# A graph-attention kernel: the values' stride in the second layer, the accumulator's second half in the third

## The chip, the core and the metric

The program runs on one NeuronCore of a Trainium2 chip. The metric is the device time of one execution in microseconds; the median of three runs is compared. A profiled execution of the same program supplies the trace. Its engines are named PE (TensorE, matmuls) with PEld (its weight loads), DVE (VectorE), ACT (ScalarE), POOL (GpSimd) and SP (SyncE, which here only issues transfers).

## What is computed

4096 nodes with 256 features each and a 0/1 adjacency matrix of 4096 x 4096 go through three graph-attention layers, a dense block of 30 steps after the first of them, and a mixture of experts at the end:

```python
x = x + _L0_gnn_ref(_layernorm(x), adj, W, a1, a2)          # attention, layer 1
x = x + _L0_ffn_ref(_layernorm(x), ...)                     # 30 dense steps
x = x + _L1_gnn_ref(t, _layernorm(x), adj, W1, a1, W2, a2)  # attention, layers 2 and 3
x = x + _L1_ffn_ref(_layernorm(x), ...)                     # experts, top 2 of 6
```

One attention layer, for each of four heads of 64 columns:

```python
h = jnp.einsum('nf,hfd->hnd', x, W)
f1 = jnp.einsum('hnd,hd->hn', h, a[:, :D])
f2 = jnp.einsum('hnd,hd->hn', h, a[:, D:])
e = jax.nn.leaky_relu(f1[:, :, None] + f2[:, None, :], ALPHA)
e = jnp.where(adj[None, :, :] > 0, e, NEG)
att = jax.nn.softmax(e, axis=-1)
out = jax.nn.elu(jnp.einsum('hnm,hmd->hnd', att, h))
```

## The kernel before

The leaky relu has two branches, and the exponential of a sum is a product. So the softmax-weighted sum over the neighbours m of a node n splits into two sums: one over the neighbours with f1 + f2 above zero, one over those below it. Each neighbour contributes a factor that depends on m alone, which is multiplied into its values beforehand, and a factor of n alone, which is applied at the end. What is left for the matmuls is to add up rows of values under two 0/1 masks, "above" and "below".

**Values.** The tile `vals` holds, for each block j of 128 neighbours and each head h, two parts (above and below). A part is 130 numbers of 16 bits: 65 high halves (64 columns and the denominator) and 65 low halves, which together carry more precision than one 16-bit number. Its shape before is [128, 32, 4, 2, 2, 65] (DV = 65). A part is therefore 260 bytes long, the parts lie end to end, and the second begins 260 bytes after the first. `upper` writes the high halves (ACT, L378), `lower` the low halves (DVE, L383).

**Masks.** For each block of neighbours ACT or DVE compares f1 with f2 (L462, L460) into the tile `st`. DVE then ANDs `st` with the adjacency mask (L568), which makes the mask "above", and XORs the result with the adjacency mask (L574), which makes `below`. All of these are 8-bit.

**Products (L520).** The nodes of a layer are worked in four chunks of 1024, which is 8 tiles of 128 nodes, each with its own PSUM bank of 512 numbers. A unit is one chunk, one head and four neighbour blocks. In a unit, and for each of two groups of four banks, the loop runs over the four blocks s, the four tiles i, and the two parts. Each pass loads a mask of 128 x 128 as weights and streams one part's 130 columns of values:

```python
for i in range(n):
    ...
    for part in range(2):
        cols = slice(2 * part * DV, 2 * (part + 1) * DV)
        nc.tensor.matmul(
            acc[:, i, cols], masked[part][:, at_i // TR, s, rows], v[:, cols], ...
```

So part 0 (weights `st`) goes to columns 0 to 129 of bank i, part 1 (weights `below`) to columns 130 to 259, and then the next bank follows. Each layer has 128 units of 64 matmuls: 8192 matmuls, half of them of each part. After eight units a head of a chunk is finished; `lower_sums` (ACT, L469) and `whole_sums` (DVE, L473) read the banks through the view `split`, and `close` (DVE mostly, L483 to L498) finishes the output.

**Order.** In the stage with the products, the instructions of DVE and ACT stand in the order of the program's text (`manual_schedule`). The preparation before it (the layer's projections, its scores, the values) is ordered by the scheduler, from its own estimates and from which memory is free. SP issues the loads in one queue: 1 MB adjacency masks (L193), rows of the layer's input into the tile `ring` (L93), scores (L188, L348), and stores of outputs (L628).

**Memory.** `vals` comes from a pool that is opened after a few small ones, and the pools for masks, f1, steps, work and outputs lie above it. Layers 2 and 3 open the same pools in the same order at the same addresses, so that in the kernel before a tile of layer 3 lies where the same tile of layer 2 was. The dense block, which stands between layers 1 and 2, has its own pools in the same memory.

Of the kernel before, what the change touches and what calls it, by code (L numbers as in the profile page):

```python
# [13 lines left out]
F16 = mybir.dt.float16  # L14
# [9 lines left out]
P = 128  # L24
C = 256
KC = C // P
H = 4
# [7 lines left out]
DV = D + 1  # L35
# [11 lines left out]
def gnn_ffn_kernel(ctx: ExitStack, tc: tile.TileContext, a: dict, out: bass.AP):  # L47
# [3 lines left out]
    NT = N // P  # L51
# [106 lines left out]

        return w, (load, make, centre)

    def attention(tag, src, norm, w, front, chunks, first, ends, following, side={}):

# [4 lines left out]
        with ExitStack() as scope:  # L169
# [2 lines left out]
            nf2 = lay.tile([P, NT, H], F32, name="nf2")  # L172
            hs = lay.tile([P, 1, H, DV], F32, name="hs")
            end = None if first else scope.enter_context(tc.tile_pool(name=f"{tag}_end", bufs=1))
            vals = scope.enter_context(tc.tile_pool(name=f"{tag}_vals", bufs=1)).tile(
                [P, NT, H, 2, 2, DV], F16, name="vals"
            )
            mask = [scope.enter_context(tc.tile_pool(name=f"{tag}_mask", bufs=4))]
            fpool = scope.enter_context(tc.tile_pool(name=f"{tag}_f", bufs=2))

# [55 lines left out]
            with ExitStack() as ps:  # L236
# [164 lines left out]
                for g in range(NG + 2):  # L401
                    if g + 2 < NG:
                        load(g + 2)
                    if 2 <= g < NG:
                        columns(g)
                    if 1 <= g <= NG:
                        now = products(g - 1)
                    if 2 <= g:
                        lower(g - 2)
                    if g < 2:  # L410
                        columns(g)
                    if g in (0, 2) and late:
                        late.pop(0)()
                    if 1 <= g <= NG:
                        upper(g - 1, *now)
                    if first:
                        for n in range(PREP * g // 8, min(PREP * (g + 1) // 8, PREP)):
                            make_piece(n)
                    elif g in (2, 4, 6):
                        load_mask(0, g // 2)  # L420
# [41 lines left out]
                    nc.scalar.activation(out, f1, AF.Sign, bias=f2, scale=-1.0)  # L462

            def split(acc, n):
                return acc[:, :n, : 4 * DV].rearrange("p i (b s c) -> p i b s c", b=2, s=2)

            def lower_sums(i0, n, acc):
                lo = end.tile([P, 4, 2, DV], F32, name="lo", bufs=2)
                nc.scalar.activation(lo[:, :n], split(acc, n)[:, :, :, 1, :], AF.Copy, scale=1.0 / LOW)  # L469
                return lo  # L470

            def whole_sums(u, lo, i0, n, acc):
                nc.vector.tensor_tensor(  # L473
                    u[:, i0 : i0 + n], split(acc, n)[:, :, :, 0, :], lo[:, :n], OP.add
                )
# [28 lines left out]
            pairs = {}  # L504

            def products(at, k):


                c, h, q = units[at]
                masked = pairs[at]  # L510
                for s in range(JU):
                    j = JU * q + s
                    v = vals[:, j, h].rearrange("p b s c -> p (b s c)")
                    i0, n, acc = accs[c, h][k]
                    for i in range(n):
                        at_i = (i0 + i) * P
                        rows = slice(at_i % TR, at_i % TR + P)
                        for part in range(2):
                            cols = slice(2 * part * DV, 2 * (part + 1) * DV)
                            nc.tensor.matmul(  # L520
                                acc[:, i, cols],
                                masked[part][:, at_i // TR, s, rows],
                                v[:, cols],
                                start=(j == 0 and part == 0),
                                stop=(j == NT - 1 and part == 1),
                                skip_group_check=True,
                            )
# [10 lines left out]
            with tc.manual_schedule(engines={mybir.EngineType.DVE, mybir.EngineType.Activation}):  # L538
# [3 lines left out]
                for at in range(len(units) + LAG):  # L542
                    b = at - LAG
# [4 lines left out]
                    if at < len(units):  # L548
                        c, h, q = units[at]
# [26 lines left out]
                    if b >= 0:  # L576
                        for k in range(2):
                            if bq == 0:
                                space(bc, bh, k)
                            products(b, k)  # L580
                        pairs.pop(b)
                        if not first and bh == H - 1 and bq % 2 == 1 and bc + 1 < len(chunks):
                            load_mask(bc + 1, bq // 2)
                        if 0 < bq < 7 and closing is not None:
                            next(closing)
# [16 lines left out]
            c, h, q = units[-1]  # L602
# [6 lines left out]
    def to_rows(dst, src=None):  # L609


        def block(x, t, n, h):
            return x[t * P : (t + n) * P, h * D : (h + 1) * D].rearrange("(r p) d -> p r d", p=P)

        def begin(t, n, h, work):
            if src is not None:
                old = work.tile([P, 4, 2, DV], F32, name="old", tag="lo", bufs=2)
                old = old.rearrange("p i b c -> p (i b c)")[:, : 8 * D].rearrange("p (i d) -> p i d", d=D)
                nc.sync.dma_start(old[:, :n], block(src, t, n, h))
                return old[:, :n]  # L620

        def finish(t, n, h, u, e, old):
            if src is None:
                nc.vector.tensor_scalar(u, u, 0.0, -1.0, op0=OP.max, op1=OP.add)
            else:
                nc.vector.scalar_tensor_tensor(u, u, 0.0, old, op0=OP.max, op1=OP.add)
            made = nc.vector.scalar_tensor_tensor(e, e, 1.0, u, op0=OP.min, op1=OP.add)
            nc.sync.dma_start(block(dst, t, n, h), e)  # L628
            return made

        return begin, finish
# [106 lines left out]
    first = ctx.enter_context(tc.tile_pool(name="f_first", bufs=4))  # L738
# [49 lines left out]
    def front(prep, small_ps):  # L788
# [12 lines left out]
    side = {  # L801
        31: [(begin_weights, 1)],
        28: [(load, g) for g in range(3)],
        26: [(make_weights, 1, 0)],
        22: [(make_weights, 1, 1)],
        20: [(load, 3)],
        18: [(measure, 0)],
        14: [(measure, 1)],
        10: [(rate, 0), (rate, 1)],
        4: [(measure, 2)],  # L810
        1: [(measure, 3), (init, 0), (init, 1), (rate, 2), (rate, 3)],
    }
    attention(
        "g0",
        x,
# [176 lines left out]
    def centre_weights(prep, small_ps):  # L992
        layers[1][1][2](small_ps)

    side = {
        k: functools.partial(many, v)
        for k, v in {24: (begin_weights, 2), 14: (make_weights, 2, 0), 10: (make_weights, 2, 1)}.items()
    }
    for n in range(2):
        attention(  # L1000
            f"g{n + 1}",
            h1d if n else x2d,
            not n,
            layers[n + 1][0],
            None if n else centre_weights,
            [8, 8, 8, 8],
            False,
            to_rows(x3d, x2d) if n else to_rows(h1d),
            [NG // 2, x3d, runs_of] if n else [2, h1d],
            {} if n else side,  # L1010
        )


# [5 lines left out]
    with ExitStack() as scope:  # L1019
# [4 lines left out]
        acc = one.tile([P, NT, C], F32, name="acc")  # L1024
# [256 lines left out]
        with tc.tile_pool(name="r_ps", bufs=1, space=PSUM) as psum, tc.tile_pool(  # L1281
            name="r_pst", bufs=4, space=PSUM
# [11 lines left out]
            for i in range(3):  # L1294
                src = a[f"L1_ffn_expert_w{i + 1}"]
# [173 lines left out]
```

## Time and profile before

| | us |
|---|---|
| median of 3 runs (2987.83 to 2989.67) | 2988.52 |
| profiled execution: its own time | 2978.01 |
| profiled execution: span of the trace | 2976.1 |
| products of layer 1, first to last start (L520) | 93.2 to 599.4 |
| products of layer 2 | 1624.2 to 2112.0 |
| products of layer 3 | 2166.4 to 2652.4 |
| experts, after layer 3 | 2652 to 2976 |

The span is the distance from the first to the last instruction of the trace. The dense block and the preparation of layer 2 fill the time from 600 to 1624 us, and the preparation of layer 3 the 54 us between the products of layers 2 and 3. Over the whole span PE is busy for 94%, DVE for 92% and ACT for 83%, but these are averages over stages with different limits, so each stage has to be read by itself. The mean granted TensorE clock is 0.979 of full speed; it is 1.00 in the middle of each attention layer.

### The profile page before, as it was taken

How to read it: one execution, taken by the hardware profiler on the slowest of the kernel's cores; microseconds unless marked ns; L12 is line 12 of the kernel's file. 1: busy time of each engine (PE TensorE's matmuls, PEld its weight loads, DVE VectorE, ACT ScalarE, POOL GpSimd, SP SyncE). 2: the span in 40 equal slices, each digit the busy share in tenths (PEclk: the TensorE clock that was granted, in tenths of full speed). 3: DMA queues.
4: the chain of work that ended last, by engine and by line, in shares of the span. 5: the costliest groups of instructions: out<-in, count | busy, mean ns of one | idle time of the engine just before them, and what ended most of it. 6: DMA issues, size and time to landing. Idle time of an engine off the chain costs nothing. (4 is left out here: it accounts for less than half of the span.)

```text
span 2976.1 us, 82659 instructions
## 1 busy us (share of the span) xinstructions
PE 2800.0 (94%) x33923; PEld 2562.3 (86%) x33923; DVE 2740.5 (92%) x5769; ACT 2465.1 (83%) x3125; POOL 1157.6 (39%) x1084
## 2 busy tenths in 40 slices
PE   7899999979999999999998999999889999986996
PEld 5899999968888888888887999999789999975995
DVE  7999999999999999999998899999889999986775
ACT  6799999988888888888877999999789999963342
POOL 3000000079999999999982000000200000014663
PEclk9999999989999999999999999999999999997998
DMA  9998885053333333333353031121302132124253
GB/s 292 272 255 243 227 239 154 24 128 68 68 68 68 68 69 68 68 67 70 68 111 119 22 102 57 64 80 34 108 23 91 55 104 88 44 78 147 81 173 135
DMA packets 484451, 320.07 MB, mean 108 GB/s; under 512 B 416590, under 2 KB 445419, under 8 KB 477931
## 3 DMA queue, kind: packets, MB, share of 16 engines
q1 hardware_dynamic: 474034, 290.27, 36.3%
q0 software_dynamic: 7104, 19.41, 2.1%
q8 instruction: 268, 4.39, 0.6%
q10 hardware_dynamic: 2936, 5.11, 0.5%
q14 instruction: 109, 0.88, 0.1%
HBM read 183.00 MB, written 52.04 MB: 79 GB/s over the span
## 5 line engine op out<-in xcount | busy, mean ns | idle before, releaser
L520 PE MATMUL acc<-vals,st 128*128 128x130 f16 x12288 | 1433.2, 218 | 38.3 <-DVE u L473 29.9
L520 PE MATMUL acc<-vals,below 128*128 128x130 f16 x12288 | 1432.9, 221 | 12.8 <-DVE below L574 12.0
L462 ACT ACTIVATE st<-f1b,nf 128x1024 int8<-128x1024 f32 x1265 | 1334.8, 1143 | 33.4 <-PE acc L520 24.1
L520 PEld LDWEIGHTS <-below 128*128 128x128 fp8e4 x12288 | 1176.5, 96 | 52.9 <-issue 46.5
L520 PEld LDWEIGHTS <-st 128*128 128x128 fp8e4 x12288 | 1208.2, 98 | 9.4 <-DVE st L568 7.5
L936 PE MATMUL po<-wT,zT 128*128 128x256 f32 x1920 | 576.1, 382 | 5.8 <-DVE y L876 3.2
L939 PE MATMUL po<-w,zT 128*128 128x256 f16 x3840 | 578.0, 273 | 0.7 <-DMA zT<-z 0.7
L907 POOL TENSOR_TENSOR th<-th,y 128x1024 f32<-128x1024 f32 x232 | 549.1, 2367 | 14.9 <-DVE z_st L916 0.4
L939 PEld LDWEIGHTS <-zT 128*128 128x128 f16 x3840 | 376.7, 98 | 162.0 <-DMA zT<-z 1.4
L574 DVE TENSOR_TENSOR below<-m,st 128x1024 int32<-128x1024 int32 x384 | 470.0, 1224 | 32.6 <-DVE st L568 0.9
L568 DVE TENSOR_TENSOR st<-st,m 128x1024 int32<-128x1024 int32 x384 | 467.3, 1217 | 0.2
L876 DVE SCALAR_TENSOR_TENSOR y<-po,z_rs,bias 128x256 f32<-128x256 f32 x928 | 384.4, 477 | 1.8 <-PE tp L868 0.7
L916 DVE BATCH_NORM_STATS2 z_st<-z 128x6 f32<-128x256 f32 x960 | 335.8, 413 | 0.0
L936 PEld LDWEIGHTS po<-wT,zT 128*128 128x128 f32 x1920 | 291.1, 192 | 15.3 <-ACT zT L923 3.6
L892 ACT ACTIVATE z<-th 128x1024 f32<-128x1024 f32 x240 | 251.7, 1049 | 17.5 <-POOL th L907 16.7
L927 POOL TENSOR_TENSOR z_rs<-z_rs,mhalf 128x4 f32<-128x4 f32 x240 | 244.6, 1019 | 3.1 <-ACT z_rs L926 3.1
L906 ACT ACTIVATE th<-y 128x1024 f32<-128x1024 f32 x232 | 241.7, 1042 | 0.0
L923 ACT COPY zT<-tp 128x512 f32<-128x512 f32 x240 | 140.4, 585 | 90.8 <-PE tp L868 89.7
L460 DVE TENSOR_SCALAR st<-f1b,nf 128x1024 int8<-128x1024 f32 x271 | 201.2, 743 | 7.6 <-PE acc L520 7.6
L759 POOL TENSOR_TENSOR x_rs<-x_rs,mhalf 128x4 f32<-128x4 f32 x8 | 9.4, 1174 | 503.6 <-ACT x_rs L758 503.6
L1044 POOL IOTA along_i<- 128x512 int32 (+1 forms) x5 | 2.8, 556 | 486.7 <-PE acc L520 486.6
L437 POOL MEMSET hs<- 128x4 f32 x3 | 0.3, 99 | 492.8 <-DVE u L490 492.8
(263 smaller groups left out, 3158.8 us busy)
## 6 DMA issues: line engine op xcount, KB each, us to landing
ring<-in_adj_dram SPq DMA_DIRECT2D x64, 1024.0 KB
m<-edges SPq DMA_DIRECT2D x32, 1024.0 KB
f1b<-fd SPq DMA_DIRECT2D x48, 512.0 KB
edges<-m SPq DMA_DIRECT2D x16, 1024.0 KB
y<-yd SPq DMA_DIRECT2D x16, 512.0 KB
ew<-in_L_ffn_expert_w_dram SPq DMA_DIRECT2D x18, 256.0 KB
t<-in_x_dram SPq DMA_DIRECT2D x8, 512.0 KB
old<-in_x_dram SPq DMA_DIRECT2D x16, 256.0 KB
```

The lines of the kernel that those rows point to most:

```text
L462: nc.scalar.activation(out, f1, AF.Sign, bias=f2, scale=-1.0)
L520: nc.tensor.matmul(acc[:, i, cols], masked[part][:, at_i // TR, s, rows], v[:, cols], start=(j == 0 and part == 0), stop=(j == NT - 1 and ...
L568: nc.vector.tensor_tensor(above, above, whole, OP.bitwise_and)
L574: nc.vector.tensor_tensor(below, whole, above, OP.bitwise_xor)
L876: nc.vector.scalar_tensor_tensor(t[:, r, :] if end else y[:, g * G + r, :], po[:, r, :], rstd[:, r : r + 1], t[:, r, :] if end else bias, ...
L892: ins = nc.scalar.activation(z, th.pop(u), AF.Silu, scale=0.01)
L906: nc.scalar.activation(th[at], was, AF.Tanh, scale=0.01)
L907: ins = (nc.gpsimd if at else nc.vector).tensor_tensor(th[at], th[at], was, OP.add)
L916: nc.vector.bn_stats(st[:, r, :], z[:, r, :])
L927: nc.gpsimd.tensor_tensor(rs[u], rs[u], mhalf, OP.pow)
L936: nc.tensor.matmul(po[:, r, :], src[:, r * P : (r + 1) * P], wT, start=True, stop=False)
L939: nc.tensor.matmul(po[:, r, :], src16[:, part * G + r, :], w16[:, other, :], start=False, stop=(part == 1 and other == 1),)
```

## The change

`attention` gets an argument `apart` of two strides. The first is the distance between the parts of `vals`, in 16-bit numbers: 2 * DV = 130 before, 160 in layer 2 after the change (320 bytes, with 60 bytes unused after each part). The second is the column of the bank at which part 1 of the accumulator begins: 2 * DV = 130 before, 256 in layer 3 after the change. Layer 1 keeps both at 130; layer 2 keeps the accumulator's, layer 3 the values'.

```diff
-    def attention(tag, src, norm, w, front, chunks, first, ends, following, side={}):
+    def attention(tag, src, norm, w, front, chunks, first, ends, following, side={}, apart=(2 * DV, 2 * DV)):
...
-            vals = scope.enter_context(tc.tile_pool(name=f"{tag}_vals", bufs=1)).tile(
-                [P, NT, H, 2, 2, DV], F16, name="vals"
-            )
+            apart_v, apart_s = apart
+            values = scope.enter_context(tc.tile_pool(name=f"{tag}_vals", bufs=1)).tile(
+                [P, NT, H, 2, apart_v], F16, name="vals"
+            )[:, :, :, :, : 2 * DV]
+            vals = values.rearrange("p t h b (s c) -> p t h b s c", s=2)
...
             def split(acc, n):
-                return acc[:, :n, : 4 * DV].rearrange("p i (b s c) -> p i b s c", b=2, s=2)
+                pairs = acc[:, :n, : 2 * apart_s].rearrange("p i (b c) -> p i b c", b=2)
+                return pairs[:, :, :, : 2 * DV].rearrange("p i b (s c) -> p i b s c", s=2)
...
-                    v = vals[:, j, h].rearrange("p b s c -> p (b s c)")
...
-                            cols = slice(2 * part * DV, 2 * (part + 1) * DV)
                             nc.tensor.matmul(
-                                acc[:, i, cols],
+                                acc[:, i, part * apart_s : part * apart_s + 2 * DV],
                                 masked[part][:, at_i // TR, s, rows],
-                                v[:, cols],
+                                values[:, j, h, part],
...
             {} if n else side,
+            (2 * DV, 256) if n else (160, 2 * DV),
         )
```

In the last hunk n is 0 for layer 2 and 1 for layer 3. The number of instructions of each kind and their sizes stay as they are. `vals` of layer 2 grows from 66,560 to 81,920 bytes in each partition, and the pools above it move up by 15,360 bytes, in layer 2 alone.

## The prediction

> **What bounds the kernel now.** I read first the page's costliest groups, then the busy time of each engine in the middle of layers 2 and 3, then the list for the products' line, and last the start times that the trace records for these matmuls, to the nanosecond.
>
> ```profile
> PE 2800.0 (94%) x33923; PEld 2562.3 (86%) x33923; DVE 2740.5 (92%) x5769; ACT 2465.1 (83%) x3125; POOL 1157.6 (39%) x1084
> ...
> L520 PE MATMUL acc<-vals,st 128*128 128x130 f16 x12288 | 1433.2, 218 | 38.3 <-DVE u L473 29.9
> L520 PE MATMUL acc<-vals,below 128*128 128x130 f16 x12288 | 1432.9, 221 | 12.8 <-DVE below L574 12.0
> ```
>
> The mean of 218 or 221 ns is how long one matmul is in flight. They overlap, so the price of one is the distance to the next start.
>
> ```profile
> core 0: us, PE busy (x) PEld busy (x) DVE busy (x) ACT busy (x) POOL busy (x), PEclk, DMA share, GB/s
> 1650.00:2100.00 450.00, 443.98 (x7656) 441.69 (x7654) 419.40 (x473) 422.85 (x428) 0.00 (x0) 1.00 0.18 59
> 2190.00:2640.00 450.00, 445.60 (x7690) 443.64 (x7687) 421.26 (x468) 423.43 (x429) 0.00 (x0) 1.00 0.22 68
> ```
>
> In both layers PE is busy for 99% at full clock, DVE and ACT for 93 to 94%. PE sets the end of these stages, and what a matmul costs is paid 8192 times in each; but the cover below it is only 6% thick.
>
> ```profile
> L520 PEld LDWEIGHTS <-st x12288: 95/98/152, 93.2 to 2652.3; 128*128 128x128 fp8e4 x199
> L520 PE MATMUL acc<-vals,st x12288: 217/218/315, 93.2 to 2652.3; 128*128 128x130 f16 x199
> L520 PEld LDWEIGHTS <-below x12288: 95/95/152, 94.5 to 2652.3; 128*128 128x128 fp8e4 x199
> L520 PE MATMUL acc<-vals,below x12288: 220/221/315, 94.6 to 2652.4; 128*128 128x130 f16 x199
> ```
>
> This list gives shortest, median and longest. Two matmuls of the same size differ by 3 ns, and the weight load that runs under the second part (that of `st`) by as much. The start times say it better. From a first part to the next start it is 55.83 ns, from a second part 59.46 ns, in layers 1, 2 and 3 alike; a pair costs 115.29 ns. In layer 2 the 8131 gaps under 64 ns sum to 468.7 us of 487.8, in layer 3 to 468.7 of 485.9; the rest is stalls.
>
> What makes the second part dearer? The first is 55.83 ns (within 0.03) for all heads and both parities of the block, though its start in memory moves by 8 bytes from head to head. After stalls it is again the second part that is dear, whichever came first. So the difference belongs to the part, not to a rhythm. A second part differs in four things: values that start 260 bytes later, sums that start at column 130, other weights, and a change of bank behind it. The last is free elsewhere: in the dense block (L939, 256 columns) the gap is 109.1 to 109.2 ns, with and without a change of bank. The weights of both parts have the same shape and come from tiles 4096 bytes long. That leaves the two addresses, and the change moves one of them in each layer.
>
> **The change part by part.**
>
> *Nothing added in count.* DVE's and ACT's operations on `vals` (L383 1234 ns, L378 1082 ns) and on the banks (L473 697 ns, L469 599 ns) keep their sizes; only the step between their runs of 65 changes. I cost that at 0. If each took 1% more, 32 of 1.2 us and 64 of 0.65 us in a layer would add under 1 us to engines that are not the bound.
>
> *Layer 2, values at 320 bytes.* The second part now starts like the first, at a multiple of 64 bytes from it. No row shows such a second part, so I bound it. If the address of the values is the cause, a second part falls to the first's 55.83: 4096 x 3.63 = 14.9 us gained. A smaller gain comes from a rule: the Trainium skill ("TensorE: Matmul & The Clock Gate", section "Wait — 56ns, not 53.3ns?") puts a warm gap at N / 2.4 + 2.5 ns. The dense row agrees, 109.2 for 256 columns. For 130 it gives 56.7, which no part here shows: the first is below it, the second above. Read as a mean it makes a pair 113.3 ns, and the gain 4096 x 1.95 = 8.0 us. If the address is not the cause, the gain is 0.
>
> *Layer 3, part 1 at column 256.* The same bounds by the same rows: 14.9 us, 8.0 us or 0.
>
> *A rule that speaks against both.* The Trainium skill ("SBUF — State Buffer", section "Door 1: The DMA port swizzle (why `[64,N]` ≈ `[32,N]`)") gives SBUF lines of 16 bytes and PSUM lines of 8, with a price for each new line. A run of 260 bytes touches 17 lines from any start that occurs here, at stride 260 and at 320; the sums at column 130 (byte 520) already begin a PSUM line. By the rule both edits are worth 0. It could be worse: at stride 260 the last line of the first part is also the first of the second, so that a pair touches 33 lines, and 34 at stride 320. The rows fit neither reading well: a start that moves by 8 bytes would change the filling of lines, and the first part doesn't notice. I take the rows.
>
> *What takes the gain back.* In the two windows DVE is busy for 421 of 450 us at most and ACT for 423. With 64 matmuls a unit falls from 64 x 57.65 = 3.69 us to 3.57 (3%), DVE and ACT then stand at 97%. PE stays the bound, but their bursts at the end of a head (L473, L483 to L495) will make it wait more often; the 17 to 19 us of stalls may grow by a few. I leave 11 of 14.9, which is also about the middle of 8.0 and 14.9. I take it for **one layer only**, since one cause explains the 3.63 ns.
>
> *The moved pools.* Layer 3's first two mask buffers now lie where the end of layer 2's values was. Their loads, which stand early in SP's queue, must wait for PE's last products instead of DVE's last use of the masks. The order of SP's queue is changed accordingly: the first mask, a row load, the second mask, two row loads, the third, and the fourth before the scores.
>
> ```profile
> 2105.38 0.33 SPq L193 DMA_DIRECT2D m<-edges  x1
> ...
> 2106.86 1.64 SPq L193 DMA_DIRECT2D m<-edges  x3
> 2114.78 0.37 SPq L93 DMA_DIRECT2D ring<-h1d  x1
> ```
>
> Behind the waiting mask stand row loads that PE holds back until the same time (2114.8), so they lose nothing; they even come ahead of 3 MB of masks. The first mask is used at 2143.9 (L568), 32 us after the products end. That use is now later in DVE's order; two comparisons (L460) move by an instruction or two as well. The preparation is DVE's, some 5.5 us for each of eight groups, and its last instruction stays. I cost it at 0, between -1 and +3. Before layer 2 the values now lie over rows that the dense block stores last. Those stores are issued at 1566.2, the first value is written at 1577.7: 0.
>
> **Sum.** 2978.0 - 11 = 2967 for the profiled execution. The median of the runs is 10.5 us above it; the change is taken over: 2988.5 - 11 = **2977.5 us**.
>
> **The rivals.**
>
> 1. *No change.* The price lies in 130 columns as such: a pair at 115.3 ns is about 2 x 132 columns plus the overhead, as if each run were rounded up to a multiple of 4; and the unequal gaps are only where the start is stamped. Or both addresses must be right together, and no layer has both. For it speaks the rule of lines; against it, that the gap keeps to the part after stalls. 2988.5, with the pools 2985 to 2993.
>
> 2. *Slower: a shared line is lost.* The short gap is short because the second part goes on where the first stopped, in values or in sums; the line at the seam is then paid once for a pair. Apart, each part pays for its own, and both take the long gap: 4096 x 3.63 = 14.9 us. By columns: from 55.83 ns at 130 to 109.18 at 256 a column costs 0.42 ns, a line of eight 3.4, together 13.9 us. It decides as soon as one layer's pair is over 115.3 ns, since PE is the bound and nothing covers it: 3002.4 to 3003.4. For it speaks that the first part is cheaper than the rule's 56.7; against it, that heads with another filling of the lines show the same.
>
> 3. *Both layers gain*, if a seam in either place costs: 2 x 11 = 22, 2966. One cause for one difference speaks against it.
>
> **How the numbers follow.** One layer gains: 0.38. Both: 0.04. No change: 0.26. Slower: 0.32, of which a few hundredths are a lost 6 to 10 us between the layers by transfers that collide. A change under 0.2% (6 us) can't be told from none. Faster by more 0.42, within 0.26, slower by more 0.32. The forecast's own range is 2972 to 2981 (14.9 with stalls up, or down to 8.0). With the cases of the other sign the range goes from 2972 to 3003; both layers at once, and two lines lost at once, are left out.
>
> **What would show it.** Right: in one of layers 2 and 3 the matmuls of `below` fall from 221 to 218 ns with `st`'s weight loads from 98 to 95, its products shorten by 8 to 15 us, DVE's and ACT's shares rise to 96 or 97%; layer 1 stays at 55.8 and 59.5 ns. Wrong: the gap is unchanged in both (rival 1), or the first part rises to the second's (rival 2), or the 54 us between the layers' products change by more than 3.

## The result, and the profile after

The change makes the kernel faster by 0.23%: the ratio of the times is 0.9977, with a 95% interval from 0.9972 to 0.9983. The medians of 18 runs each are 2983.38 us after and 2988.91 us before, measured together; they differ by 5.5 us, and their quotient alone, 0.9981, also lies in the interval.

The gain is in the products of layer 2: the price of a matmul is unchanged in the other two layers. This is the products' line by duration (shortest, median and longest in ns), first in the middle of layer 2 of the kernel after, then in the middle of its layer 3:

```profile
L521 PE MATMUL acc<-vals,st x3883: 217/220/220, 1649.8 to 2099.9; 128*128 128x130 f16 x195
L521 PE MATMUL acc<-vals,below x3883: 217/220/231, 1649.8 to 2100.0; 128*128 128x130 f16 x195
L521 PEld LDWEIGHTS <-st x3882: 95/98/99, 1650.0 to 2100.0; 128*128 128x128 fp8e4 x195
L521 PEld LDWEIGHTS <-below x3881: 95/98/98, 1650.0 to 2099.9; 128*128 128x128 fp8e4 x195
```

```profile
L521 PE MATMUL acc<-vals,below x3845: 220/221/222, 2189.8 to 2640.0; 128*128 128x130 f16 x193
L521 PE MATMUL acc<-vals,st x3844: 217/218/219, 2189.9 to 2639.9; 128*128 128x130 f16 x193
L521 PEld LDWEIGHTS <-st x3844: 97/98/99, 2190.0 to 2640.0; 128*128 128x128 fp8e4 x193
L521 PEld LDWEIGHTS <-below x3843: 95/95/97, 2190.0 to 2639.9; 128*128 128x128 fp8e4 x193
```

In layer 3 the list is as it was: 218 ns for a first part, 221 for a second. In layer 2 both now stand at 220, and their weight loads, 98 and 95 before, both at 98. The second part has become cheaper and the first dearer, and 55 more matmuls of each kind fit into the same 450 us. The start times say it more finely. Gaps here are the means of all distances between starts under 66 ns:

| gap after a first part / a second part, pair (ns) | before | after |
|---|---|---|
| layer 1 | 55.84 / 59.46, 115.30 | 55.84 / 59.46, 115.29 |
| layer 2 | 55.83 / 59.46, 115.29 | 56.66 / 56.66, 113.32 |
| layer 3 | 55.84 / 59.45, 115.29 | 55.84 / 59.45, 115.29 |

The stages of the two profiled executions:

| us | before | after |
|---|---|---|
| products of layer 2 | 487.8 | 480.9 |
| of these, gaps under 66 ns / stalls | 468.7 / 19.1 | 460.7 / 20.2 |
| from there to the products of layer 3 | 54.4 | 52.4 |
| products of layer 3 | 485.9 | 485.1 |
| experts, from layer 3's last start to the span's end | 323.8 | 335.8 |
| span | 2976.1 | 2982.0 |

The span of this one execution is longer than that before, although the medians say the opposite. The experts' stage accounts for it: 12 us more, with the same instructions in the same order; besides, the products of layer 2 begin 3.6 us later. In the profiled executions of the ten kernels below the experts took 320 to 323 us every time, so the 335.8 is not a property of the change. It need not be an accident of that execution either: its own time, 2983.79 us, is close to the median of the 18 runs after, while the profiled execution before (2978.01) is shorter than each of the 18 runs before (2985.41 at least). So the longer stage may belong to all runs of that group, before and after. No profile of the kernel before was taken in that group, and the cause stays open.

The cover under PE has become thinner, as the busy times in the two windows show (each engine's busy time and number of instructions):

```profile
core 0: us, PE busy (x) PEld busy (x) DVE busy (x) ACT busy (x) POOL busy (x), PEclk, DMA share, GB/s
1650.00:2100.00 450.00, 443.13 (x7766) 440.57 (x7763) 424.00 (x477) 426.06 (x432) 0.00 (x0) 1.00 0.19 59
2190.00:2640.00 450.00, 445.61 (x7689) 443.65 (x7687) 421.69 (x469) 420.34 (x426) 0.00 (x0) 1.00 0.22 67
```

In layer 2 PE gets through 7766 matmuls in 450 us where it was 7656; in layer 3 the number is the same to within one. DVE and ACT rise to 94 and 95% in layer 2, and PE is a little less busy, 443.1 against 444.0 us: it waits somewhat more for them.

### The profile page after: what moved, and what is told of

Same layout as the page of the kernel before. It is cut to its first block, busy times and chain, and to the rows that moved or that the text cites. A ratio compares the mean times of both kernels' runs of the same rounds, so it can differ in the third digit from the quotient of the medians.

```text
span 2982.0 us, 82665 instructions
## 1 busy us (share of the span) xinstructions
PE 2795.9 (94%) x33923; PEld 2553.5 (86%) x33923; DVE 2737.1 (92%) x5769; ACT 2463.9 (83%) x3125; POOL 1159.1 (39%) x1084
## 5 line engine op out<-in xcount | busy, mean ns | idle before, releaser
L521 PEld LDWEIGHTS <-below 128*128 128x128 fp8e4 x12288 | 1185.9, 97 | 55.0 <-issue 42.6
L439 POOL MEMSET hs<- 128x4 f32 x3 | 0.3, 103 | 485.9 <-DVE u L493 485.9
```

Source lines behind the costliest of these rows:

```text
L521: nc.tensor.matmul(acc[:, i, part * apart_s : part * apart_s + 2 * DV], masked[part][:, at_i // TR, s, rows], values[:, j, h, part], start ...
```

## The experiments

The edits below are against the kernel after. Unless it is said otherwise, the accumulator's second part is at column 130 in both layers. Byte positions are counted from the start of the tile of values, which is taken to lie at a multiple of 16 bytes. The traces hold no addresses, but the heads that pay in the first run fit this: from a start 8 bytes further, the other two heads would. Ten kernels were run; their expectations name theories A to F as they arose. Three of them were timed (5 to 12 executions each). The others ran once, under the profiler, and their prices are read from its start times; layer 1, which all but one of these kernels leave as it was, reads 115.29 or 115.30 ns every time.

**Which alignment, or is it a gap?** Two strides in one kernel:

```diff
-            (2 * DV, 256) if n else (160, 2 * DV),
+            (134, 130) if n else (132, 130),
```

> Accumulator at column 130 in all layers; values with a stride of 264 bytes in layer 2 and 268 bytes in layer 3. Before, a pair of parts costs 115.29 ns (55.83 + 59.46); with 320 bytes it cost 113.32 (56.66 twice). Theory A, a second part must start at a multiple of 8 bytes: layer 2 falls to 113.3 (264 is such a multiple), layer 3 stays at 115.3 (268 is not). Theory B, two parts that touch end to end disturb each other: both fall to 113.3, since there is a gap of 4 or 8 bytes in both. Theory C, starts at 64 bytes are needed: both stay at 115.3. Layer 1 stays at 115.3 in all.

Measured: layer 2 at 115.21 ns per pair, hardly below 115.29. Layer 3 fell to 114.32, and split by heads: 115.3 in heads 0 and 2, 113.3 in heads 1 and 3. All three theories fall: a start at a multiple of 8 bytes gains nothing, a gap of 4 bytes gains nothing, and at 268 bytes half of the heads gain it all, far from 64 bytes. What divides the heads at 268 bytes is this. In heads 0 and 2 the first part fills bytes 0 to 259 and the second starts at 268, in the same 16 bytes (256 to 271). In heads 1 and 3 everything lies 8 bytes further: the first ends at 267, and the second starts at 276, in the next 16. The gap between the parts is 8 bytes in all four heads. The place where one part ends and the next begins is called the seam from here on.

**Strides of 272 and 262 bytes:**

```diff
+            (131, 130) if n else (136, 130),
```

> Accumulator at column 130 in all layers; values with a stride of 272 bytes in layer 2 and 262 bytes in layer 3. Theory A (multiples of 8 bytes): layer 2 at 113.3 ns per pair; in layer 3 the second part is off in all heads, the first in every other head, so it stays at 115.3 or goes above, and heads 0 and 2 differ from 1 and 3. Theory B (parts that touch): 113.3 in both, no difference between heads. Theory C (64 bytes): 115.3 in both.

Measured: 272 bytes give 113.32 in all heads, 56.66 for each part. At 262 bytes the pair costs 116.0, 114.6, 116.8 and 116.0 ns in heads 0 to 3. In head 1 alone the first part ends on the last byte of 16 and the second starts in the next; it is again the cheapest. Why it is above 113.3 is not shown. Starts that are 2 bytes off a multiple of 4 occur in no other run; but what head 1 pays stands in the gap of the first part (57.91 ns, and 56.66 for the second), which starts 12 bytes into 16, and such starts come up again below.

**Late starts without contact.** The parts get an offset of their own within a slot:

```diff
+            values = [both[:, :, :, part, shift[part] : shift[part] + 2 * DV] for part in range(2)]
...
+            (144, 130, 2, 0) if n else (160, 130, 2, 2),
```

> The parts of the values no longer touch, but start 4 bytes late: in layer 2 both parts (stride 320 bytes), in layer 3 the first part alone (stride 288 bytes, the second part at a multiple of 8). Theory A with a price for each late start: layer 2 about 2 x 59.5 = 118.9 ns per pair or, if what a pair loses is 1.97 ns for the one late part, 113.3 + 2 x 1.97 = 117.3; layer 3 115.3 with the roles changed, the first part long and the second short. Theory B: 113.3 in both layers, 56.66 for each part.

Measured: layer 2 113.32 (56.66 twice) with both parts 4 bytes late, layer 3 113.32 (57.08 and 56.24) with the first part late. So the second part's own start is not what costs. A start 4 bytes into 16 is free, as long as the neighbour in time doesn't end in those 16 bytes.

**The column with the right stride:**

```diff
+            (144, 130) if n else (160, 256),
```

> Layer 2 with values at 320 bytes and the accumulator's second part at column 256, layer 3 with values at 288 bytes and column 130. If the column counts once the values are right: layer 2 falls below 113.3 ns per pair, to 111.7 (twice 55.83). If it never counts: 113.3. Layer 3: 113.3 if multiples of 8 bytes suffice (theory A) or a gap does (theory B); 115.3 if 64 bytes are needed (C), as 288 is half a step of 64. The products of both layers then take about 8 us less each than before, 16 together.

Measured: 113.32 in both layers. Column 256 gains nothing with the right stride either, and 288 bytes are as good as 320. The products take 481.0 and 478.3 us.

**The seam at a boundary, and another order.** In layer 2 both parts are placed so that the first ends and the second begins at a multiple of 16 bytes; in layer 3 only the loop is turned round:

```diff
+                    passes = [(i, part) for i in range(n) for part in range(2)]
+                    if tag in ('g2',):
+                        passes = [(i, part) for part in range(2) for i in range(n)]
+                    for i, part in passes:
...
+            (130, 130) if n else (144, 130, 14, 0),
```

> The runs so far leave: (B) parts that touch end to end disturb each other; (D) a seam costs where the second part's first bytes lie in the same 16 bytes as the first part's last ones (264 bytes kept the price, 272 lost it, at 268 it went for every other head). Layer 2: both parts moved so that the first ends and the second begins at a multiple of 16 bytes, with no gap between them. B: 115.3 ns per pair. D: 113.3. Layer 3: stride 260 as before, but in each block of neighbours first the first parts of four tiles, then their second parts. D: such a seam now comes once in eight matmuls, so 113.32 + 1.97 / 4 = 113.8 ns for two matmuls. A price of the second part's own address would stay at 115.3.

Measured: layer 3 113.79, where theory D's sum gives 113.81, with no address changed. That is the clearest result: the second part's address, its weights and its column are those of before, and the price has gone from three of four of them. Layer 2 came to 114.30, half way: theory D's 113.3 was wrong there, and so was B's 115.3.

**The stride in both layers, timed:**

```diff
+            (136, 130) if n else (136, 130),
```

> Values with a stride of 272 bytes in layers 2 and 3, accumulator at column 130. Theory D (no shared 16 bytes): both layers at 113.32 ns per pair, 8 us less in the gaps of each, 1 to 2 us of it given back in stalls: 13 to 15 us less than before, ratio 0.9950. If only one layer can gain (DVE and ACT become the bound in the other): 7 us, ratio 0.9977.

Measured: ratio 0.9949, interval 0.9936 to 0.9963; the median of 5 runs is 2962.78 us against 2977.07 before in the same group of runs. Both layers are at 113.32 ns, and their products take 481.0 and 479.1 us. This beats both kernels: the change itself stands at 0.9977. The products' line in the middle of its layer 3:

```profile
L521 PE MATMUL acc<-vals,st x3902: 217/220/220, 2189.8 to 2639.9; 128*128 128x130 f16 x196
L521 PE MATMUL acc<-vals,below x3901: 217/220/220, 2189.9 to 2639.9; 128*128 128x130 f16 x196
```

Both are at 220 ns, as in layer 2 of the kernel after, and there are 56 or 57 more of each than with the column alone moved (3845).

**The column alone:**

```diff
+            (130, 256) if n else (130, 130),
```

> The change's third-layer part alone: accumulator at column 256 in layer 3, values at 260 bytes in all layers. If the column is worth nothing: 115.3 ns per pair in all three layers, ratio 1.000 within 0.001. If it gives or costs something that the other part hid: a ratio off 1 by more than that.

Measured: ratio 1.0001, interval 0.9992 to 1.0010, and 115.29 ns in all layers. The busy times in both windows are those of the kernel before:

```profile
1650.00:2100.00 450.00, 444.01 (x7656) 441.71 (x7654) 419.47 (x473) 422.87 (x428) 0.00 (x0) 1.00 0.18 59
2190.00:2640.00 450.00, 445.62 (x7690) 443.66 (x7688) 421.29 (x467) 423.42 (x428) 0.00 (x0) 1.00 0.22 68
```

The counts of matmuls, 7656 and 7690, are the same as before to the last one. The third-layer half of the change is worth nothing.

**The order alone, in all layers, timed.** The turned loop of layer 3 in the run with the seam at a boundary, now for all three layers, with strides of 260 bytes throughout:

> No address changed: stride 260 and column 130 in all layers, but in all three layers the first parts of four tiles and then their second parts. Theory D: 113.8 ns for two matmuls in all layers, 4096 x 1.48 = 6.1 us less in the gaps of each of layers 2 and 3, 12 us together, with 2 to 3 us given back in stalls: ratio 0.9965 to 0.9970. Layer 1 gains little, as ACT is its bound (393 of 400 us busy). If only addresses count: 1.000.

Measured: ratio 0.9970, interval 0.9958 to 0.9981, and 113.79 ns for two matmuls in every layer. Layer 1 shows what a cheaper matmul is worth where PE is not the bound. Its window before, and in this run:

```profile
100.00:600.00 500.00, 477.18 (x8142) 471.70 (x8139) 483.05 (x551) 480.48 (x492) 8.29 (x12) 1.00 0.72 198
```

```profile
100.00:600.00 500.00, 472.66 (x8118) 467.12 (x8116) 481.83 (x541) 479.87 (x491) 6.97 (x10) 0.99 0.72 199
```

DVE and ACT are the busiest engines in both, and no more matmuls are done. The gaps under 66 ns fell from 463.6 to 454.9 us (46 fewer of them, 2.6 us, are under 66 ns), the stalls rose from 42.6 to 52.3, and the products took 507.2 us against 506.1. In the ten other profiled executions, whose layer 1 is that of before, they took 503.9 to 510.1 us. So no gain is seen there, though one of two or three us would not have been seen either.

**What is left at the boundary.** Neither parts that touch nor shared 16 bytes, but starts 12 bytes into a line (16 bytes from a multiple of 16):

```diff
+            (152, 130, 0, 14) if n else (160, 130, 14, 14),
```

> The run with the seam at a 16-byte boundary halved the price (114.30 ns per pair) where theory D said none. There the first part starts 12 bytes into its 16, and the second follows without a gap. Theory E: a start 12 bytes into its line, with only two numbers left in it, has a price of its own of 0.98 ns, shared line or not. Theory F: what is left comes from following without a gap. Here no parts touch or share 16 bytes (strides 320 and 304 bytes): in layer 2 both parts start 12 bytes into a line, in layer 3 the second part alone. E: 113.32 + 1.96 = 115.3 in layer 2 and 114.3 in layer 3. F: 113.3 in both.

Measured: 113.32 in layer 2, 114.18 in layer 3. Theory E falls with layer 2, theory F with layer 3. The two layers that are half dear, this one and that with the seam at a boundary, have one thing in common: of the two parts one starts at the first byte of 16 and the other 12 bytes into them. A start of 12 in both is free, and so are 4 with 0 and 8 with 4. One reading fits these layers. The longer gap is that of the part that starts 12 bytes into a line: 58.40 ns for the second part here, 58.46 for the first with the seam at a boundary, 57.91 for the first in head 1 at 262 bytes. In these three the part before it ends 4 or 6 bytes into another line; with both parts 12 bytes late it ends with the last byte of a line, and nothing is paid. No run was made to test this, and why it costs stays open.

**The second part first:**

```diff
+                    if tag == "g1":
+                        passes = [(i, part) for part in (1, 0) for i in range(n)]
+                    if tag == "g2":
+                        passes = [(i, part) for i in range(n) for part in (1, 0)]
...
+                            start=(j == 0 and part == int(not first)),
+                            stop=(j == NT - 1 and part == int(first)),
```

`first` is true in layer 1 alone; the flags that open and close a bank's sum move to the part that now comes first and last.

> All addresses as before (stride 260, column 130). Layer 2: in each block of neighbours the second parts of four tiles and then their first parts. Layer 3: per tile the second part and then the first. If only a first part directly followed by the second of the same 260 bytes pays (theory D): layer 2 never meets that seam and falls to 113.3 ns for two matmuls with no padding at all; layer 3 meets it once in two matmuls as before, from one tile to the next, and stays at 115.3. If the address of the second part has a price of its own: 115.3 in both. If changing weights tiles and banks in another order matters: neither number.

Measured: layer 2 113.43, with all addresses as before. Layer 3 114.77 where I wrote 115.3. I had miscounted: the first tile of each block of neighbours follows a first part of another block, so three seams in four are left, and 113.32 + 1.97 x 3 / 4 = 114.80. With that the seam accounts for both layers but for the 0.11 ns by which layer 2 is above 113.32. Those come from heads 1 and 3 alone (113.56 and 113.53, against 113.33 and 113.32 in heads 0 and 2), where a second part starts 12 bytes into a line after a first part that ended 12 bytes into another. That would agree with the reading of the run before; but layer 3 has the same start once in a block, and there heads 1 and 3 are dearer than 0 and 2 by 0.1 ns at most. So this stays open too.

The gaps by place say where the price is paid. A block of neighbours has eight matmuls in succession; these are the mean gaps after each of them (ns, "1" for a first part, "2" for a second, * for a part that follows a seam):

| run | | | | | | | | |
|---|---|---|---|---|---|---|---|---|
| order alone, layer 2 | 1: 56.67 | 1: 56.66 | 1: 56.65 | 1: 56.65 | 2*: 60.81 | 2: 55.87 | 2: 55.81 | 2: 56.05 |
| second part first, layer 3 | 2: 55.94 | 1: 56.06 | 2*: 60.77 | 1: 55.83 | 2*: 59.35 | 1: 55.89 | 2*: 59.40 | 1: 55.83 |

The second parts all have the addresses of before, and only those with a seam before them have the long gap. The short gaps behind it give part of it back, so that a price has to be read from the sum: in the upper row the last four exceed 4 x 56.66 by 1.9 ns. Uneven gaps alone are no price. In layer 2 of the run with the second part first, head 0, where no seam is met, the eight gaps begin with 58.31, 55.69, 56.00 and 56.55, and sum to 453.3 = 8 x 56.66.

The readings of all layers in one view:

| values (bytes) | end of first part and start of second in the same 16 bytes | pair (ns) |
|---|---|---|
| 260 | yes | 115.29 |
| 264 | yes | 115.21 |
| 268, heads 0 and 2 / 1 and 3 | yes / no | 115.3 / 113.3 |
| 262, heads 0, 2, 3 / 1 | yes / no | 116.0, 116.8, 116.0 / 114.6 |
| 272, 288, 320 | no | 113.32 |
| 320, both 4 late / both 12 late | no | 113.32 |
| 288, first 4 late | no | 113.32 |
| 304, second 12 late | no | 114.18 |
| 288, seam on a boundary | no, touching | 114.30 |
| 260, four first parts, four second parts | in one of four | 113.79 |
| 260, four second parts, four first parts | never in succession | 113.43 |
| 260, second then first, tile by tile | in three of four | 114.77 |

## Why the prediction was right, and where it was not

**The bound** was read rightly: PE sets the end of layers 2 and 3, and 8.0 us less in the gaps of layer 2 arrive as 6.9 in the length of its products. With two layers (the stride of 272) it is a ratio of 0.9949, so DVE and ACT don't take the bound over. They stand at 94 and 95% in layer 2, where I said 96 or 97.

**The two addresses as the cause, one layer gains.** Right: layer 2 gains, layer 3 nothing. The reason given, that the price belongs to the second part's address, was not right. The runs with late starts, with another order and with the second part first show that it belongs to a succession: a matmul whose values begin in the same 16 bytes in which those of the one before it ended. The start times before the change had shown that the gap keeps to the part after stalls; I took that for a property of the part, and it was one of its neighbour. That one layer gained was in part luck. The edit was made for a start at a multiple of 64 bytes; it helped because 320 bytes also put the two ends into different 16 bytes, as 272 bytes do. What I said would show it was not met either: `below` fell from 221 to 220 ns and not to 218, `st` rose from 218 to 220, the weight loads of `st` stayed at 98, and the products shortened by 6.9 us where I said 8 to 15.

**The size** is the step that failed. I took 11 us between the bounds of 14.9 and 8.0. The gaps gave 8.0 (468.7 to 460.7), the lower bound, and stalls took 1.1 of it; between the medians it is 5.5, and 2983.38 us lies above the forecast's own range of 2972 to 2981, though inside the range with the other cases. The term that was too large is the price of a pair: 3.63 ns in the upper bound, 1.97 measured. That bound supposed that the second part falls to the first's 55.83 ns. But the first part's short gap was the other side of the same seam: with the seam gone it rose to 56.66. The rule that I quoted from the Trainium skill ("TensorE: Matmul & The Clock Gate", section "Wait — 56ns, not 53.3ns?") gives 130 / 2.4 + 2.5 = 56.67 for 130 columns, and 56.66 is measured at strides of 272, 288 and 320 bytes, though not where one part alone starts 12 bytes into a line. I had held against it that no part showed it; its mean over a pair was the right reading. With 8.0 and the stalls the forecast would have been 2981.6.

**The rule of lines.** I had weighed the 16-byte lines of the same skill ("SBUF — State Buffer", section "Door 1: The DMA port swizzle (why `[64,N]` ≈ `[32,N]`)") and set them aside, because the first part didn't change when its start moved by 8 bytes. That could not tell: at a stride of 260 bytes the seam lies inside one line in every head, between bytes 259 and 260 or 267 and 268. The runs agree with the page in the size of the line. Its price for each new line they leave untested, since a part touches 17 lines in all of them but one (the second part in head 2 at 262 bytes touches 18, and that head is the dearest, at 116.8 ns). What costs is a line that two matmuls in succession share.

**Rival 2** had the seam, with the sign reversed: it supposed that a shared line is paid once, and it costs extra instead. It was given 0.32, the largest of the rivals, on the strength of one oddity, that 55.83 is below the rule; as the gaps by place show, a short gap can be the other side of a long one beside it. Why a pair's time is split unevenly stays open.

**The stalls and the pools.** Stalls in layer 2 rose from 19.1 to 20.2 us where I allowed for a few. The time between the layers' products went from 54.4 to 52.4 us, where I said 0 and -1 to +3, so it lies outside; in the other kernels it is 52 to 59 us, and I read nothing into it.

## What to carry to other kernels

Where matmuls are short and PE is the bound, look at the distances between starts part by part, not at the mean, and compare the sum over a pattern with the rate of matmuls elsewhere in the trace; a short gap beside a long one may be one price seen from two sides. If two matmuls in succession stream neighbouring runs of SBUF, give the runs a stride that is a multiple of 16 bytes, or order them so that such neighbours don't follow each other: here each was worth up to 2 ns for every pair. Where there is no memory for padding the order does it. In layer 1, which PE doesn't bound, the order gained nothing that could be seen.

## What the runs showed of the hardware that was not expected

- A matmul of 130 16-bit columns whose values begin in the 16 bytes in which the values of the one before ended costs 1.97 ns more per pair (115.29 against 113.32) where the runs touch, and about as much where they lie 4 bytes (115.21) or 8 bytes (115.3) apart.
- Without such a seam the pair costs 113.32 ns with both parts 0, 4 or 12 bytes into 16, and as much with starts of 4 and 0 or of 8 and 4.
- Two parts of which one starts at the first byte of 16 and the other 12 bytes into them cost 0.9 to 1.0 ns more per pair (114.18 and 114.30), with no shared 16 bytes; the cause is open.
- The column at which a matmul writes in its bank, 130 or 256, makes no difference (115.29 both ways, and 113.32 both ways).
